# Four-layer convolution network: experts with additions to output blocks on GpSimd, the norm's pow as a step of its own, the last two block sums on VectorE, and a later third transposition

## The chip, the cores and the metric

The kernel runs on one core of one Trainium2 chip, in one launch. The metric is the device time of an execution in microseconds (us), the median of the runs. In the text PE is TensorE, DVE is VectorE, ACT is ScalarE, POOL is GpSimd, and SP is SyncE, which issues most DMAs.

## What is computed

The input x has the shape (8, 384, 32, 32) in float32. Four layers follow each other, each of the form x = x + layer(gn(x)), with gn a group norm over 32 groups of 12 channels. Layer 0 is an attention with eight heads behind depthwise projections, layer 2 a depthwise 7x7 convolution, layer 3 three fused branches. The change lies in layer 1, the experts:

```python
def _L1_conv_ref(x, gate_w, gate_b, w1, b1, w2, b2):
    E, HID, K = (4, 384, 2)
    ...
    scores = jax.nn.softmax(x_flat @ gate_w + gate_b, -1)
    top_v, top_i = jax.lax.top_k(scores, K)
    top_w = jax.nn.softmax(top_v, -1)
    wmap = top_w.T.reshape(K, b, h, w)
    present = (top_i[:, :, None] == jnp.arange(e)[None, None, :]).any(0)
    coef = jnp.einsum('ke,kbhw->ebhw', present.astype(x.dtype), wmap)
    hdn = jax.nn.relu(jnp.einsum('bchw,edc->ebdhw', x, w1) + b1[:, None, :, None, None])
    y = jnp.einsum('ebdhw,eod->ebohw', hdn, w2) + b2[:, None, :, None, None]
    return jnp.einsum('ebohw,ebhw->bohw', y, coef)
```

`present` holds, for each rank k and expert e, whether any token of the batch chose e at rank k. Where all are present, the coefficients of a token add up to one for every expert, and the output is the plain sum over the four experts. The kernel computes that sum, checks the gates, and has a second path for the other case.

## The kernel before

The experts take the eight images one after the other, each in two halves h = 0 and h = 1 of 512 tokens. In this part PE, ACT, DVE and POOL each follow the order in which the program issues their instructions, and an instruction that waits holds everything behind it on its engine. SP's DMAs are ordered by the scheduler.

A half has two parts. In the **dual part** the hidden values of three experts (e = 0, 1, 2) are made by a scheme with fewer products: a 384x384 matrix times 384x512 values is cut in 3x3 blocks of weights and 3x2 blocks of values of 256 columns, and 15 block products ("nodes", table `DUAL`) replace 18. Each node is one product (L1295, two instructions) of a sum of weight blocks (`w1sum`) and a sum of value blocks (`forms`, made by POOL at L1276 for the half after). Its result `p` lies in one of five PSUM banks, and the additions listed with the node (L1304, DVE) put it into the output blocks of `hs` or into scratch nodes, which lie in the fourth expert's slot of `hs_sum`. Nodes 14 and 10 are copied out by ACT (L1301). After nodes 6 and 5 ACT applies bias and Relu to a finished block row (`rectify`, L352). The fourth expert is done in the plain way (`classical`, L1314, ACT at L1324), its instructions strewn between the nodes.

In the **products part** the second matrix product runs over all four experts by another such scheme: 15 products (`PRODUCTS`, L1344), each accumulated over the four experts in one of the same five banks, on blocks of `hs` or on block sums (`HSUMS`, L1337), and added by DVE to two or so blocks of the residual r (L1353, L1355). The first eight block sums of `HSUMS` are made by POOL, for expert e - 1 right after the dual of expert e, for the last dual expert and the fourth at once after the dual part. The last two, over all four experts, use slots that come free in the products; they follow after product 8, on POOL for h = 0 and on DVE for h = 1 (both on DVE in the first image).

Other work is hung on the products as jobs: `jobs[i]` runs after product i is issued. In h = 0 these are the steps of `passing`, the norm of the image before (moments by `bn_stats`, L250; `centred`, L311 to L313; the group matmul, L304; `norm2`, which calls `from_moments` with four DVE steps, a pow on POOL at L332 and a step on DVE at L337; then for each of three channel tiles an affine step on ACT, a transposition on DVE at L1014, two pad copies on POOL and a store by SP), the normalizing of the next half (`normed`), the forms of the next half (`make_forms`, twelve additions on POOL) and the loads of the next image (`fetch_next`). In h = 1 they are the next image's residual (L1164), its `normed` and its forms.

The first half of the first image is different. All four experts are done in the plain way, in the order 3, 0, 1, 2, the block sums are on DVE, and POOL makes the sums of weight blocks, `WSUMS` of w2 (L1248) and then of w1 (`sum_weights`, L1262).

Of the kernel before, what the change touches and what calls it, by code (L numbers as in the profile page):

```python
# [64 lines left out]
def taps(xp, dy, dx, rows=H, h0=0):  # L65
# [72 lines left out]
    (0, (((0, 0), "p0", 9, 1),)),  # L138
    (9, ((8, 11, "p9", -1), ((0, 0), (0, 0), 11, 1))),
    (11, ((6, "p11", 9, 1), ((1, 0), (1, 0), 8, 1))),  # L140
    (8, ((3, "p8", 8, 1),)),
    (3, (((0, 1), "p3", 6, 1), ((1, 1), (1, 1), 3, 1))),
    (7, ((10, 6, "p7", -1), (10, 10, 3, 1))),
    (2, (((2, 0), "p2", 10, 1),)),
    (6, (((0, 1), (0, 1), "p6", 1), ((2, 1), "p6", 10, 1))),
    (5, (((1, 1), (1, 1), "p5", 1), ((2, 1), (2, 1), "p5", 1))),
)
NODE_AT = {n: i for i, n in enumerate((1, 9, 6, 10, 14, 11, 8, 3))}
READY = {6: (0,), 5: (1, 2)}
# [24 lines left out]
def conv_mixer_kernel(ctx: ExitStack, tc: tile.TileContext, a: dict, out: bass.AP):  # L174
# [139 lines left out]

    def from_moments(own, ps, ref, s, t, gm, first=None):

        c, n = ps.shape[1], ps.shape[3]
        both, sq = (
            own.tile([P, c, n], FP, tag=f"fm_{k}", name=f"fm_{k}") for k in "ab"
        )  # L320
        nc.vector.tensor_copy(both, ps[:, :, 0])
        nc.vector.tensor_mul(sq, both, both)
        nc.vector.scalar_tensor_tensor(
            out=sq, in0=ps[:, :, 1], scalar=EPS, in1=sq, op0=ALU.add, op1=ALU.subtract
        )
        nc.vector.tensor_add(gm, both, ref)
        for n0, n1 in ((0, first or n), (first or n, n)):
# [4 lines left out]
            nc.gpsimd.tensor_tensor(  # L332
                out=s[:, :, n0:n1], in0=sq[:, :, n0:n1], in1=half, op=ALU.pow
            )
            if n0:
                yield
            nc.vector.scalar_tensor_tensor(  # L337
                out=t[:, :, n0:n1], in0=gm[:, :, n0:n1], scalar=-1.0, in1=s[:, :, n0:n1],
                op0=ALU.mult, op1=ALU.mult,
            )  # L340
# [250 lines left out]
    def layers(again, early, xst, pre_pool, pp0, pw):  # L591
# [548 lines left out]
        def experts():  # L1140
# [100 lines left out]

            def block(n):
                if isinstance(n, tuple):
                    return w2[:, :, n[1], n[0] * P : (n[0] + 1) * P]
                return wsum[:, wslot[n]]

            for o, i, sign, j in WSUMS:
                nc.gpsimd.tensor_tensor(  # L1248
                    out=block(o), in0=block(i), in1=block(j), op=ALU.add if sign > 0 else ALU.subtract
                )  # L1250
            w1slot = {n: i for i, n in enumerate(n for n in wslot if n not in (8, 9))}
# [7 lines left out]
            def sum_weights(some):  # L1259
                for o, i, sign, j in some:  # L1260
# [4 lines left out]
                    )  # L1265

            def form_of(n, xn):
                n = PLAIN.get(n, n) if isinstance(n, int) else n
                if isinstance(n, tuple):
                    return xn[:, n[0], n[1] * QF : (n[1] + 1) * QF]  # L1270
                return forms[:, fslot[n]]

            def make_forms(xn):
                for o, i, j, sign in FORMS:
                    i, j = (form_of(v, xn) for v in (i, j))
                    nc.gpsimd.tensor_tensor(  # L1276
                        out=forms[:, fslot[o]], in0=i, in1=j,
                        op=ALU.add if sign > 0 else ALU.subtract,
                    )
# [3 lines left out]

            def dual(hs, e, xn, part, got):

# [7 lines left out]
                for n, ops in DUAL[part]:  # L1293
                    ps = got[f"p{n}"] = ep.tile([P, HF], FP, tag="p", name="p")
                    nc.tensor.matmul(  # L1295
                        ps[:, :QF], lhsT=block1(PRODUCTS[n][0])[:, e], rhs=form_of(n, xn),
                        start=True, stop=True,
                    )
                    for o, i, *more in ops:
                        if not more:  # L1300
                            nc.scalar.copy(at(o), at(i))  # L1301
                            continue
                        j, sign = more
                        nc.vector.tensor_tensor(  # L1304
                            out=at(o), in0=at(i), in1=at(j), op=ALU.add if sign > 0 else ALU.subtract
                        )
                    for m in READY.get(n, ()):
                        rectify(hs, e, m)
# [26 lines left out]
            def sums(hs, some, s, eng=nc.vector):  # L1335
                for o, i, j in some:
                    eng.tensor_add(rows_of(o, hs, s), rows_of(i, hs, s), rows_of(j, hs, s))  # L1337

            def products(b, h, hs, jobs):
                r, begun = rs[b], set()  # L1340
                for i, (w, x, outs) in enumerate(PRODUCTS):
# [36 lines left out]

            def norm2(ps, b, cos, st):
                c = slice(cos[0], cos[-1] + 1)  # L1380
                cols = [st[:, c, i : i + 1] for i in range(3)]
                for _ in from_moments(er, ps[:, c], ref2[:, c, b : b + 1], *cols):
                    pass

            def next_layer(b):
# [3 lines left out]
                if b < B - 1:  # L1389
# [21 lines left out]
                for i, (cts, co) in enumerate(zip(parts, cos)):  # L1411
# [7 lines left out]
                    yield  # L1419
                    norm2(ps, b, co, st)  # L1420
                    yield
# [29 lines left out]
            for b, h in product(range(B), range(2)):  # L1451
# [1111 lines left out]
```

## Time and profile before

| What | us |
|---|---|
| time before, median of 3 runs | 3171.03 (3170.06 to 3171.54) |
| the profiled execution's own time | 3177.68 |
| its span | 3175.9 |
| busy PE, DVE, ACT, POOL over the span | 3001.4, 1912.0, 1213.5, 787.4 |
| first and last product of the experts (L1344) | 1765.8, 2668.5 |
| DVE additions of the dual part (L1304), one | 0.40 to 0.97 |
| POOL sums of two 128x256 blocks (L1337), median | 0.73 to 0.79 |
| POOL pow (L332), median | 0.86 |
| DVE transposition (L1014), median | 1.98 |

Times of instructions and positions come from the one profiled execution, whose time lies 6.65 us above the median. In a row of the timeline the columns are start, duration, engine, line, instruction, output and inputs, and how many instructions the row joins; in brackets stands the idle time before it and what ended it. A matmul row's duration is modelled; the distance of two starts is not.

### The profile page before, as it was taken

To read this page: it belongs to the slowest core of one execution; us is meant where nothing else is said; L and a number is where in the kernel's file an instruction comes from. 1 tells how busy PE (TensorE), PEld (TensorE's weight loads), DVE (VectorE), ACT (ScalarE), POOL (GpSimd) and SP (SyncE) were. 2 spreads that over 40 slices of the span, in tenths; PEclk is the share of its full clock that TensorE was granted. 3 is DMA by queue.
4 is the path that set the end of the run, shared out by engine and by line. 5 is a ranking of instruction groups with operands and counts; after the bars stand their busy time and mean duration, and the time that the engine had idled before them with its cause. 6 is when DMAs were issued, how large, how long until landed. Compare 5 with 4: busy or idle time off the path is not lost.

```text
span 3175.9 us, 45058 instructions
## 1 busy us (share of the span) xinstructions
PE 3001.4 (95%) x18280; PEld 1696.7 (53%) x18280; DVE 1912.0 (60%) x3179; ACT 1213.5 (38%) x1446; POOL 787.4 (25%) x982
## 2 busy tenths in 40 slices
PE   4988999999999999999998999999999999887998
PEld 3765434343433334343433677777777777556543
DVE  6898354445444444445445778878877876447164
ACT  3654453535445353535342122212222223446510
POOL 2432000000000000000001565575665663111400
PEclk9999999999999999999999999999999999898999
DMA  6787011011101111011004012112112114867765
GB/s 218 270 278 288 37 38 67 23 62 43 60 25 60 43 43 62 23 62 43 13 23 163 1 40 84 44 40 84 54 39 76 51 41 143 321 221 241 235 221 188
DMA packets 89105, 323.02 MB, mean 102 GB/s; under 512 B 13608, under 2 KB 16000, under 8 KB 84664
## 3 DMA queue, kind: packets, MB, share of 16 engines
q1 hardware_dynamic: 64936, 251.71, 23.3%
q10 hardware_dynamic: 13776, 35.82, 3.6%
q0 software_dynamic: 10176, 32.51, 3.0%
q8 instruction: 146, 2.39, 0.3%
q14 instruction: 71, 0.58, 0.1%
HBM read 211.66 MB, written 111.68 MB: 102 GB/s over the span
## 4 chain that ended last, share of the span: by engine, by line
PE 74%; DVE 14%; DMA 5%; issue 3%; POOL 2%; ACT 1%; SPq 0%; ACTq 0%; DVEq 0%; POOLq 0%
PE sc L771 15%; PE av L790 14%; PE p L1344 10%; PE p L1295 8%; PE sc L669 7%; PE sc L724 4%; PE sc L846 4%; PE ph L1314 4%; DVE stats L250 3%; DVE y L499 2%; DVE hs L1304 2%; PE po L2374 1%; PE po L2377 1%; PE po L2385 1%; DVE xt L466 1%
## 5 line engine op out<-in xcount | busy, mean ns | idle before, releaser
L778 ACT ACTIVATE e<-sc 128x1024 f32<-128x1024 f32 x512 | 483.1, 1029 | 609.1 <-PE sc L771 608.9
L771 PE MATMUL sc<-qT,kT 64*128 64x512 f32 x2048 | 473.9, 602 | 0.0
L790 PE MATMUL av<-e,vT 128*64 128x512 f32 x2048 | 467.7, 598 | 0.0
L771 PEld LDWEIGHTS sc<-qT,kT 64*128 64x128 f32 x2048 | 186.7, 186 | 282.1 <-issue 231.2
L790 PEld LDWEIGHTS av<-e,vT 128*64 128x64 f32 x2048 | 135.5, 136 | 316.4 <-issue 316.4
L820 POOL DMA_DIRECT2D att<-att x45 | 23.8, 533 | 980.7 <-DVE att L815 980.7
L806 DVE LOAD_MASK_SELECT sm<-av x64 | 0.9, 14 | 417.0 <-PE av L790 417.0
L1337 POOL TENSOR_TENSOR hs_sum<-hs,hs_sum 128x256 f32<-128x256 f32 (+1 forms) x239 | 247.1, 1042 | 14.7
L669 PE MATMUL sc<-y,pw 128*128 128x512 f32 x576 | 249.3, 594 | 0.0
L528 PE MATMUL ps<-xt,wx 64*64 64x256 f32 x3456 | 197.3, 386 | 38.3 <-DVE xt L466 21.4
L808 DVE RECIPROCAL inv<-sm 128x512 f32<-128x512 f32 x64 | 214.6, 3353 | 2.2
L352 ACT ACTIVATE hs<-hs,b 128x512 f32<-128x512 f32 x135 | 89.8, 716 | 293.4 <-DVE hs L1304 293.4
L1337 POOL TENSOR_TENSOR hs_sum<-hs 128x256 f32<-128x256 f32 (+1 forms) x135 | 132.9, 1013 | 271.6 <-ACT hs L352 214.3
L528 PEld LDWEIGHTS ps<-xt,wx 64*64 64x64 f32 x3456 | 155.4, 137 | 79.1 <-issue 37.5
L1353 DVE TENSOR_TENSOR r<-r,p 128x256 f32<-128x256 f32 x416 | 152.9, 412 | 67.9 <-PE p L1344 64.7
L1295 PE MATMUL p<-forms,w 128*128 128x256 f32 x630 | 178.5, 391 | 8.4 <-DVE hs_sum L1304 6.3
L1114 PE MATMUL ps<-xt,wx 64*64 64x256 f32 (+1 forms) x2912 | 161.1, 380 | 24.9 <-ACT wx L1716 14.5
L669 PEld LDWEIGHTS sc<-y,pw 128*128 128x128 f32 x576 | 108.8, 190 | 140.0 <-issue 138.6
L1344 PE MATMUL p<-hs_sum,wsum 128*128 128x256 f32 x768 | 174.2, 380 | 0.0
L1314 PE MATMUL ph<-xn,w 128*128 128x512 f32 x342 | 159.9, 602 | 3.0 <-ACT xn L352 3.0
L1304 DVE TENSOR_TENSOR hs<-p,hs_sum 128x256 f32<-128x256 f32 x270 | 113.7, 421 | 77.5 <-PE p L1295 30.6
L1344 PEld LDWEIGHTS p<-hs_sum,wsum 128*128 128x128 f32 x768 | 145.0, 190 | 19.9
(346 smaller groups left out, 4628.3 us busy)
## 6 DMA issues: line engine op xcount, KB each, us to landing
raw<-y SPq DMA_DIRECT2D x72, 512.0 KB
y<-raw SPq DMA_DIRECT2D x24, 1536.0 KB
x<-x SPq DMA_DIRECT2D x23, 608.0 KB
xt<-x SPq DMA_DIRECT2D x23, 608.0 KB
w<-in_w ACTq DMA_DIRECT2D x36, 384.0 KB
xn<-in_x SPq DMA_DIRECT2D x24, 512.0 KB
x<-in_x SPq DMA_DIRECT2D x16, 768.0 KB
z<-z POOLq DMA_DIRECT2D x16, 768.0 KB, 4.3
```

Source lines behind the costliest of these rows:

```text
L528: nc.tensor.matmul(ps[64 * d : 64 * d + 64, 2 * i + e, cc], lhsT=w[r, 12 * cc + 6 * e + 3 * d + k, :], rhs=xt0s[ct][r, 16 * d + 4 * u + 2 ...
L669: nc.tensor.matmul(ps[:, h, :], lhsT=w[:, ct, pair, :], rhs=y[:, ct, h * HF : (h + 1) * HF], start=ct == 0, stop=ct == NC - 1,)
L771: nc.tensor.matmul(sc[:, s, :], lhsT=kTs[b][r, pair, m * P : (m + 1) * P], rhs=qTs[b][r, pair, h * HF : (h + 1) * HF], start=True, stop=True,)
L778: nc.scalar.activation(e, sc, AF.Exp, scale=1.0 if shifted else HD**-0.5)
L790: nc.tensor.matmul(av[64 * s : 64 * s + 64, :], lhsT=vTs[0][:, m, c0 : c0 + 64], rhs=e[:, s, :], start=m == 0, stop=m == N // P - 1,)
L808: nc.vector.reciprocal(inv, sm)
L1114: nc.tensor.matmul(ps[64 * d : 64 * d + 64, 2 * i + e, c % 2, images], lhsT=w[r, d * K7 + k, :], rhs=by_slot(xts[ct])[r, 16 * d + column(c ...
L1295: nc.tensor.matmul(ps[:, :QF], lhsT=block1(PRODUCTS[n][0])[:, e], rhs=form_of(n, xn), start=True, stop=True,)
L1304: nc.vector.tensor_tensor(out=at(o), in0=at(i), in1=at(j), op=ALU.add if sign > 0 else ALU.subtract)
L1314: nc.tensor.matmul(ph, lhsT=w1[:, e, ct, dc * P : (dc + 1) * P], rhs=xn[:, ct, :], start=ct == 0, stop=ct == NC - 1,)
L1337: eng.tensor_add(rows_of(o, hs, s), rows_of(i, hs, s), rows_of(j, hs, s))
L1344: nc.tensor.matmul(ps[:, :QF], lhsT=block(w)[:, e], rhs=rows_of(x, hs, e), start=e == 0, stop=e == E - 1,)
```

## The change

- `DUAL` loses three additions that read only SBUF, (0,0) += 11, (1,0) += 8 and (1,1) += 3. They stand in `ASIDE`, are issued on POOL after nodes 9, 11 and 3, and work on the expert at hand. The node order is the same.
- The eight block sums of expert e - 1 are no longer issued in one piece after the dual of expert e. A generator `sums_of` issues one of them on POOL after each of the nodes in `FILL`. Those of the last two experts stay in one piece.
- `norm2` is a generator that pauses between the pow and the step that reads it, so these are two jobs (after products 6 and 8).
- The steps of `passing` are hung on products 0, 1, 2, 3, 5, 6, 8, 10, 12 instead of 0, 1, 2, 3, 6, 7, 9, 10, 12, 14; the last one, the third transposition with its pads and store, follows the dual of expert 1 in h = 1.
- The forms of h = 1 are made in two parts, three after product 3 and nine after product 6 (behind the pow). The rest of w1's sums in the first image moves from product 4 to 7, the next image's loads from 14 to 13.
- The last two block sums are on DVE in every half.
- In the first half w1's sums are issued ahead of w2's, and DVE's block sums follow each expert by itself.

```diff
-    (9, ((8, 11, "p9", -1), ((0, 0), (0, 0), 11, 1))),
-    (11, ((6, "p11", 9, 1), ((1, 0), (1, 0), 8, 1))),
+    (9, ((8, 11, "p9", -1),)),
+    (11, ((6, "p11", 9, 1),)),
     (8, ((3, "p8", 8, 1),)),
-    (3, (((0, 1), "p3", 6, 1), ((1, 1), (1, 1), 3, 1))),
+    (3, (((0, 1), "p3", 6, 1),)),
...
+ASIDE = {9: ((0, 0), 11), 11: ((1, 0), 8), 3: ((1, 1), 3)}
+FILL = (4, 13, 1, 12, 8, 7, 6, 5)
...
-            if n0:
+            if n0 or pause:
                 yield
...
+            sum_weights(WSUMS[:8])
...
             for o, i, sign, j in WSUMS:
                 nc.gpsimd.tensor_tensor(
...
-            def make_forms(xn):
-                for o, i, j, sign in FORMS:
+            def make_forms(xn, part=slice(0, len(FORMS))):
+                for o, i, j, sign in FORMS[part]:
...
+                    if n in ASIDE:
+                        o, i = ASIDE[n]
+                        nc.gpsimd.tensor_add(at(o), at(o), at(i))
+                    if n in FILL:
+                        next(fill, None)
                     for m in READY.get(n, ()):
                         rectify(hs, e, m)
...
+            def sums_of(hs, e):
+                for some in HSUMS[:-2]:
+                    yield sums(hs, (some,), slice(e, e + 1), nc.gpsimd)
...
                     if i == 8:
-                        begun_all = b > 0 and h == 0
-                        sums(hs, HSUMS[-2:], slice(0, E), nc.gpsimd if begun_all else nc.vector)
+                        sums(hs, HSUMS[-2:], slice(0, E))
...
-                    norm2(ps, b, range(NC), st)
-                    yield
+                    yield from norm2(ps, b, range(NC), st, True)
...
-                        if e == E - 3:
-                            for s in (slice(E - 1, E), slice(0, E - 2)):
-                                sums(hs, HSUMS[:-2], s)
-                    sums(hs, HSUMS[:-2], slice(E - 2, E - 1))
-                    sum_weights(WSUMS[:8])
+                        sums(hs, HSUMS[:-2], slice(e, e + 1))
...
-                        dual(hs, e, xn, slice(2, len(DUAL)), got)
-                        if e:
-                            sums(hs, HSUMS[:-2], slice(e - 1, e), nc.gpsimd)
+                        fill = sums_of(hs, e - 1) if e else iter(())
+                        dual(hs, e, xn, slice(2, len(DUAL)), got, fill)
+                        if (h, e) == (1, 1) and passing:
+                            next(passing, None)
...
-                        for i in (0, 1, 2, 3, 6, 7, 9, 10, 12, 14):
+                        for i in (0, 1, 2, 3, 5, 6, 8, 10, 12):
                             at(i, next, passing)
                     at(2, normed, b, 1)
-                    at(3, lambda b=b: make_forms(xns[b, 1]))
+                    at(3, lambda b=b: make_forms(xns[b, 1], slice(0, 3)))
+                    at(6, lambda b=b: make_forms(xns[b, 1], slice(3, len(FORMS))))
                     if b == 0:
-                        at(4, sum_weights, WSUMS[8:])
+                        at(7, sum_weights, WSUMS[8:])
                     if b + 1 < B:
-                        at(14, fetch_next, b + 1)
+                        at(13, fetch_next, b + 1)
```

More of the change, by code (lines that the diff above doesn't have):

```diff
@@ L313, in centred, with from_moments @@
         nc.vector.tensor_add(o[:, :, 1], o[:, :, 1], var)
-    def from_moments(own, ps, ref, s, t, gm, first=None):
+    def from_moments(own, ps, ref, s, t, gm, first=None, pause=False):
         c, n = ps.shape[1], ps.shape[3]
@@ L1240, in experts @@
             lg = ew.tile([P, NT, E], FP, name="lg")
[L1242 to L1250, printed above, removed]
             w1slot = {n: i for i, n in enumerate(n for n in wslot if n not in (8, 9))}
@@ L1265, in sum_weights, with block @@
                     )
+            sum_weights(WSUMS[:8])
+            def block(n):
+                if isinstance(n, tuple):
+                    return w2[:, :, n[1], n[0] * P : (n[0] + 1) * P]
+                return wsum[:, wslot[n]]
+            for o, i, sign, j in WSUMS:
+                nc.gpsimd.tensor_tensor(
+                    out=block(o), in0=block(i), in1=block(j), op=ALU.add if sign > 0 else ALU.subtract
+                )
             def form_of(n, xn):
@@ L1282, in rectify, with dual @@
                 affine(hs[:, m, e], hs[:, m, e], 1.0, b1[:, e, m : m + 1], AF.Relu)
-            def dual(hs, e, xn, part, got):
+            def dual(hs, e, xn, part, got, fill=iter(())):
                 def at(n):
@@ L1377, in centred2, with norm2 @@
                 )
-            def norm2(ps, b, cos, st):
+            def norm2(ps, b, cos, st, pause=False):
                 c = slice(cos[0], cos[-1] + 1)
                 cols = [st[:, c, i : i + 1] for i in range(3)]
-                for _ in from_moments(er, ps[:, c], ref2[:, c, b : b + 1], *cols):
-                    pass
+                return from_moments(er, ps[:, c], ref2[:, c, b : b + 1], *cols, pause=pause)
             def next_layer(b):
@@ L1419, in next_layer @@
                     yield
-                    norm2(ps, b, co, st)
+                    for _ in norm2(ps, b, co, st):
+                        pass
                     yield
```

## The prediction

> **What bounds the kernel now.** I read the page first: the busy line and the slices.
>
> ```profile
> span 3175.9 us, 45058 instructions
> PE 3001.4 (95%) x18280; PEld 1696.7 (53%) x18280; DVE 1912.0 (60%) x3179; ACT 1213.5 (38%) x1446; POOL 787.4 (25%) x982
> PE   4988999999999999999998999999999999887998
> DVE  6898354445444444445445778878877876447164
> POOL 2432000000000000000001565575665663111400
> ```
>
> PE sets the pace nearly everywhere. The change lies in slices 22 to 33 (the experts, 1730 to 2670 us), where DVE has digits of 7 and 8 and POOL of 5 to 7. Only PE's idle time can be won there. One image takes (2643.54 - 1944.44) / 6 = 116.52 us (starts of the piece "PE p L1344 x116" in the chain of work). The windows view of one such image:
>
> ```profile
> 1976.00:2092.00 116.00, 112.74 (x495) 86.88 (x495) 91.29 (x203) 27.72 (x46) 71.85 (x81) 1.00 0.19 57
> ```
>
> PE (first pair) looks busy for 112.74, but ends are modelled, so I count starts. Instructions on 256 columns start every 0.216 us (24 from 2072.30 to 2077.48), on 512 columns every 0.43. An image has 2 x 15 products of 8 (51.8), 2 x 45 dual products of 2 (38.9), 2 x 18 classical instructions (15.5), logits 1.43, the group matmul 1.48, the two transpositions 0.22: 109.3 us. So PE loses about 7.2 us an image. Which waits these are, PE's own waits in 1730 to 2700 say (total, times, longest):
>
> ```profile
> PE p L1344 <- DVE r L1353: 8.7, 7, 1.3
> PE p L1295 <- DVE hs_sum L1304: 6.3, 15, 0.4
> PE p L1344 <- ACT hs L352: 6.2, 15, 0.4
> PE p L1344 <- DVE r L1355: 2.6, 1, 2.6
> ```
>
> PE's timeline places them, as the excess of each stretch over its count of starts:
>
> ```profile
> 1777.17 5.41 PE L1344 MATMUL p<-hs_sum,w 128*128 128x256 f32 x16 [2.62 <-DVE r L1355]
> 1988.06 0.70 PE L1295 MATMUL p<-forms,w 128*128 128x256 f32 x2 [0.42 <-DVE hs_sum L1304]
> 2010.97 1.62 PE L304 MATMUL gn_ps<-dq,gmatA 128*128 128x2 f32 x14
> 2024.31 1.97 PE L1344 MATMUL p<-hs_sum,w 128*128 128x256 f32 x8 [1.26 <-DVE r L1353]
> 2060.97 4.58 PE L1344 MATMUL p<-hs,w 128*128 128x256 f32 x20 [0.42 <-ACT hs L352]
> ```
>
> Dual part of h=0: 1969.80 to 1998.20 is 28.4 against 27.2 counted, 1.2 lost, all in experts 1 and 2; expert 0, without block sums on POOL beside it, loses nothing. Products of h=0: 29.6 against 27.4, 2.3 lost: 0.7 before expert 2's rectified block, 1.4 at 2024.31. Dual part of h=1: 31.7 against 28.8, 2.9 lost: 1.4 in expert 0, 1.5 in experts 1 and 2. Products of h=1: 0.7, again the rectified block. Sum 7.0.
>
> DVE and POOL show why:
>
> ```profile
> 1986.71 0.96 DVE L1304 TENSOR_TENSOR hs<-hs,hs_sum 128x256 f32<-128x256 f32 x1
> 2009.36 1.19 DVE L313 TENSOR_TENSOR dq<-dq,gn_mv 128x3 f32<-128x3 f32 x1
> 2021.20 2.31 DVE L337 SCALAR_TENSOR_TENSOR st<-st 128x3 f32<-128x3 f32 x1 [4.94 <-POOL st L332]
> 2033.37 1.98 DVE L1014 STREAM_TRANSPOSE x<-xn 128x1024 f32<-128x1024 f32 x1
> ```
> ```profile
> 1982.06 2.10 POOL L1337 TENSOR_TENSOR hs_sum<-hs 128x256 f32<-128x256 f32 x3 [12.31 <-ACT hs L352]
> 1984.23 4.02 POOL L1337 TENSOR_TENSOR hs_sum<-hs,hs_sum 128x256 f32<-128x256 f32 x5
> 2020.30 0.87 POOL L332 TENSOR_TENSOR st<-fm_b,mhalf 128x3 f32<-128x3 f32 x1
> 2021.14 4.79 POOL L1337 TENSOR_TENSOR hs_sum<-hs,hs_sum 128x1024 f32<-128x1024 f32 x2
> ```
>
> In experts 1 and 2 the three additions to output blocks take DVE 0.59, 0.61 and 0.96 us instead of 0.42, because both inputs lie in SBUF while POOL adds. DVE's expert lasts 9.44 us (1982.27 to 1991.71), PE's 8.2. At 2016 to 2021 DVE stands 4.94 us for a pow that is queued on POOL behind all twelve forms, then 2.31 us on a 128x3 step behind POOL's 128x1024 sum: PE has no free bank, and its fourteenth product no sum, until 2024.31. The third transposition ends at 2035.35, when dual work has been waiting since 2033.3.
>
> **The change part by part.**
>
> *Additions to POOL.* Per expert DVE loses three instructions: 16 x 0.34 = 5.4 us remain for 13 nodes that PE makes in 5.6. Expert 0 of h=0, which kept PE free of stalls with 19 uncontended instructions, is the nearest row: I take 0 for these stalls (1.2 + 1.5). DVE is also done sooner, so ACT's rectified block is there 1 us before PE asks: the 0.7 twice an image goes too. What is queued: POOL's eight sums took 6.19 us (1982.06 to 1988.25), 0.77 each; eleven take 8.5 against PE's 8.2. POOL starts 2.3 us behind PE's end of the expert before and falls back by 0.3. DVE's last addition to (1,1) now waits for POOL's: due at 2.3 + 8 x 0.77 = 8.5 us after that end, while DVE reaches it at 9.0 (node 3 is done at 7.0, five additions of 0.34 to 0.5 follow). Nothing is late; bounds: 0 to 1 us per expert on DVE, which five banks cover up to 1.3.
>
> The Trainium skill, "GPSIMD Engine Reference", section 4.1 "Engine selection", advises VectorE for elementwise additions, GpSimd being about half as fast for two inputs. By that rule alone the three additions would cost 3 x 0.82 instead of 3 x 0.41, and the edit would lose; the rows have 0.73 to 0.80 on POOL against 0.59 to 0.96 on a DVE that is the late one.
>
> *Pow as its own step, forms in two parts.* pow now stands behind three forms (2.4 us) instead of twelve (9), and its reader comes two products later: DVE's wait of 4.94 and most of the 2.31 go, and with them 1.4 on PE.
>
> *Last two sums on DVE.* For h=0 2.9 us on DVE (the h=1 row, 2076.62 to 2079.51, also beside forms). DVE's products of h=0 then hold 10.7 (32 additions) + 4.5 (moments) + 2.6 + 1.6 + 2.9 + 4.0 (two transpositions) = 26.3 against PE's 27.4, banks in hand: hidden. If that cover is gone, it costs up to 2.9 less the slack of 1.1, 1.8 an image. The Trainium skill, "SBUF — State Buffer", section "Who interferes with whom", says that of a DVE instruction with two SBUF inputs and a GpSimd one the later is held for the whole of the earlier. By it each of the two sums may hold a form by 1.4 us. In the row, at 2076.81, two forms took 1.61 and 1.59 us instead of 0.73; the forms held are read 6 us later, so I cost this at nothing.
>
> *Third transposition after expert 1 of h=1.* DVE has there about 1.5 us between its experts and 1.3 more before PE's banks run out; 1.98 us fits. POOL's two pad copies (0.28 each) push expert 2's block sums back by 1.3 us; the final sums still begin 2.5 us after the products do, before 3.3. SP's store of that piece goes behind the next image's loads, with half an image to spare. The 1.4 in expert 0 goes, since ACT and DVE are free when it starts.
>
> *Group matmul one product earlier* (job 5 instead of 6): a new wait. DVE's chain from the first addition to the end of L313 is 2000.81 to 2010.47, 9.7 us; starting 1.85 after the products begin it ends at 11.5. PE comes there after 6 x 1.73 = 10.4. L312 and L313 each wait for POOL's running 128x512 sum; by how its boundaries fall the pair takes 1.3 to 2.4 us. So PE waits 0 to 1.4 us; I take 0.9.
>
> *First image.* Sums expert by expert, and w1's sums ahead of w2's on a POOL that idles until 1739.6: POOL ends near 1760 instead of 1767.7, so the last experts' sums on DVE run uncontended (0.35 instead of 0.9 to 1.4 each) and end near 1770 instead of 1776.3: the 2.6 us at 1777.17 go. Its second half loses 2.1 in all (55.4 from 1798.69 to 1854.07 against 53.3); 1.9 go.
>
> **Sum.** Per image 7.0 - 0.9 - 0.4 (small remainders of 0.1) = 5.7; seven images 39.9; first image 2.6 + 1.9: 44 us. The profiled execution took 3177.68 (span 3175.9 and 1.8 around it) and should become 3133; the median, 6.65 lower, becomes 3171 - 44 = 3127.
>
> **The rivals.**
> 1. POOL is held to the order of the dual and half the gain goes into new waits: the 0.9 is 1.4, DVE's 1.8 in the products shows, and 0.5 of each dual part stays. Against it: every one of these has slack above. Gain 7.0 - 1.4 - 1.8 - 1.0 = 2.8 an image, 20 and 3 for the first: 3148.
> 2. POOL paces the experts, and the kernel is slower. From expert 0's rectified block 19 POOL instructions must be done before PE reaches expert 2's block (1,0), 18.7 us later: allowed 0.98 us each, and the gain is gone at 1.14. At 1.2 each half is late by 4.1 us, 15 halves 61, less 44: 3188. For it: POOL's 128x512 sums took 1.90 instead of 1.25 beside DVE's residual steps (2062.84). Against it: with DVE busy in the same dual part they took 0.70 to 0.80, and DVE was the one held.
> 3. The steps only change places, PE's losses stay: 3171. Against it: rows name DVE and POOL as the late ones.
>
> **How the numbers follow.** Forecast 0.76 (3115 with no new wait, 53 to 56 us gained, to 3137 with 1.4 and 1 us left elsewhere), rival 1 0.14 (3137 to 3158), rival 2 0.06, rival 3 0.04. A measurement of this kernel tells 0.2%, 6.3 us. Range 3114 to 3148; faster 0.90, same 0.04, slower 0.06.
>
> **What would show it.** Right: the image's period near 110.8; no PE wait for DVE hs_sum L1304, none before the fourteenth product; a PE wait for dq of about 1 us, seven times; DVE's st step without POOL ahead of it; POOL's sums in the dual at 0.7 to 0.8. Wrong: PE waits for POOL's block sums or ACT's rectified blocks (rival 2), or for DVE's r in h=0 (rival 1).

## The result, and the profile after

The changed kernel takes 3129.79 us (median of 4 runs, 3127.23 to 3131.61) against 3171.05 us (3170.06 to 3171.54): a ratio of 0.987, with a 95% interval of 0.9853 to 0.9887. The gain is 41.3 us; forecast were 44 us, to 3127. The profiled execution took 3131.1 us with a span of 3129.4, which is 46.5 less than the span before. The profile of before lay 6.65 us above its median and this one 1.3, so 5.3 of the 46.5 belong to the executions and not to the change.

The page of the changed kernel (span, busy time, slices):

```profile
span 3129.4 us, 45250 instructions
PE 2978.0 (95%) x18280; PEld 1710.8 (55%) x18280; DVE 1857.4 (59%) x3066; ACT 1211.5 (39%) x1446; POOL 858.7 (27%) x1103
DVE  6898344445454445444445777777777776457164
POOL 2432000000000000000000577686777764111400
```

POOL has 121 instructions more and DVE 113 fewer. In the slices of the experts DVE's digits of 8 became 7, and POOL rose from mostly 5 and 6 to 6 and 7. Note where POOL stands now: in half of these slices its digit equals DVE's.

PE's own waits from 1730 to 2660, in the changed kernel (total, times, longest). Of the four groups before, none is left; this is the only one in its place:

```profile
PE gn_ps L306 <- DVE dq L315: 6.6, 8, 2.9
```

One of the eight, the 2.9, belongs to another norm at the start of the window. The other seven are the new wait that was forecast, 0.53 us each. The 2.62 us of the first half and the 1.26 before the fourteenth product are gone. PE's timeline of the changed kernel around a group matmul:

```profile
1994.01 1.70 PE L306 MATMUL gn_ps<-dq,gmatA 128*128 128x2 f32 x14 [0.53 <-DVE dq L315]
1995.57 2.83 PE L1357 MATMUL p<-hs_sum,w 128*128 128x256 f32 x8
1998.19 6.22 PE L1357 MATMUL p<-hs_sum,wsum 128*128 128x256 f32 x24
```

Look at the second line by its starts: its eight instructions need 1.73 us, and the next line starts 2.62 later. The 24 behind them take 6.05 instead of 5.18 (the line behind them starts at 2004.24). That is 1.76 us lost while PE waits for nothing. The windows of 2 us tell why (PE, PEld, DVE, ACT, POOL busy with their counts, then the granted clock, DMA share and GB/s):

```profile
1996.00:1998.00 2.00, 2.00 (x8) 1.64 (x7) 0.00 (x0) 0.00 (x0) 1.21 (x2) 0.63 0.00 0
1998.00:2000.00 2.00, 2.00 (x6) 1.53 (x6) 1.22 (x6) 0.00 (x0) 0.28 (x1) 0.51 0.00 0
2000.00:2002.00 2.00, 2.00 (x11) 1.77 (x10) 0.42 (x1) 0.00 (x0) 2.00 (x4) 1.00 0.00 0
```

From 1996.5, 0.97 us after the group matmul has ended, the granted clock is half for 3.41 us, and it returns by itself. This happens in five of the seven images. In the other two the same wait has no such sequel, as in the next image (the eight instructions behind the group matmul take 1.81 us to the next start, 2109.35):

```profile
2105.98 1.69 PE L306 MATMUL gn_ps<-dq,gmatA 128*128 128x2 f32 x14 [0.53 <-DVE dq L315]
2107.54 1.97 PE L1357 MATMUL p<-hs_sum,w 128*128 128x256 f32 x8
```

The prediction has no term for the slow stretch. The last section says what decides between the two cases.

DVE and POOL in the same half of the changed kernel:

```profile
1992.48 1.18 DVE L314 TENSOR_TENSOR dq<-dq 128x3 f32<-128x3 f32 x1
2003.39 3.38 DVE L1346 TENSOR_TENSOR hs_sum<-hs,hs_sum 128x1024 f32<-128x1024 f32 x2
2006.69 0.68 DVE L339 SCALAR_TENSOR_TENSOR st<-st 128x3 f32<-128x3 f32 x1
```
```profile
1967.64 2.10 POOL L1346 TENSOR_TENSOR hs_sum<-hs 128x256 f32<-128x256 f32 x3 [3.25 <-ACT hs L354]
1973.43 2.21 POOL L1346 TENSOR_TENSOR hs_sum<-hs,hs_sum 128x256 f32<-128x256 f32 x3
```

The eleven POOL instructions of an expert end 8.0 us after they begin, 0.73 each. DVE's step that reads pow (L339) waits for nobody and takes 0.68 (before: 4.94 of standing and then 2.31); DVE's last two sums take 3.38.

Where the span went, by starts. The group matmul is one product, 1.73 us, earlier in the changed kernel, and two rows are corrected for it:

| stretch | before | after | difference |
|---|---|---|---|
| start to the first plain product of the experts | 1732.54 | 1730.42 | -2.1 |
| from there to the first group matmul | 161.89 | 151.62 | -10.3 (-8.5 corrected) |
| six images, group matmul to group matmul | 699.11 | 668.50 | -30.6 |
| last group matmul to the end | 582.36 | 578.86 | -3.5 (-5.2 corrected) |

An image takes 110.3 us in two cases and 111.97 in the others, where the clock falls; the mean is 111.42, against 116.52 before.

### The profile page after: what moved, and what is told of

The parts are those of the page before. It is cut to its first block, busy times and chain, and to the rows that moved or that the text cites. A ratio compares the mean times of both kernels' runs of the same rounds, so it can differ in the third digit from the quotient of the medians.

```text
span 3129.4 us, 45250 instructions
## 1 busy us (share of the span) xinstructions
PE 2978.0 (95%) x18280; PEld 1710.8 (55%) x18280; DVE 1857.4 (59%) x3066; ACT 1211.5 (39%) x1446; POOL 858.7 (27%) x1103
## 5 line engine op out<-in xcount | busy, mean ns | idle before, releaser
L1346 POOL TENSOR_TENSOR hs_sum<-hs,hs_sum 128x256 f32<-128x256 f32 (+1 forms) x225 | 209.7, 940 | 9.4
L530 PEld LDWEIGHTS ps<-xt,wx 64*64 64x64 f32 x3456 | 156.8, 137 | 76.1 <-issue 39.7
L1299 PE MATMUL p<-forms,w 128*128 128x256 f32 x630 | 165.4, 379 | 0.0
L1116 PEld LDWEIGHTS ps<-xt,wx 64*64 64x64 f32 x2912 | 109.2, 139 | 73.3 <-ACT wx L1725 15.1
```

The costliest lines, as they stand in the source:

```text
L530: nc.tensor.matmul(ps[64 * d : 64 * d + 64, 2 * i + e, cc], lhsT=w[r, 12 * cc + 6 * e + 3 * d + k, :], rhs=xt0s[ct][r, 16 * d + 4 * u + 2 ...
L1116: nc.tensor.matmul(ps[64 * d : 64 * d + 64, 2 * i + e, c % 2, images], lhsT=w[r, d * K7 + k, :], rhs=by_slot(xts[ct])[r, 16 * d + column(c ...
L1299: nc.tensor.matmul(ps[:, :QF], lhsT=block1(PRODUCTS[n][0])[:, e], rhs=form_of(n, xn), start=True, stop=True,)
```

## The experiments

All kernels were timed in three rounds beside the kernel before, whose median on those chips was 3172.3 to 3173.3. "Image" is the distance of two group matmuls in the profile.

The table has the four parts of an image, by starts of PE's instructions in the profiles (us, images 2 to 8). In italics stand the values of images with half clock behind the group matmul.

| kernel | dual, h = 0 | products, h = 0 | dual, h = 1 | products, h = 1 |
|---|---|---|---|---|
| before | 28.6 | 29.6 | 31.7 | 26.6 |
| changed | 27.15 | 28.2, *29.9* | 29.0 | 25.9 |
| 1: additions back on DVE | 28.6 | 29.7, *31.3 to 33.0* | 30.7 | 26.0 |
| 3: group matmul later | 27.15 | 27.5 | 29.0 | 25.9 |
| 5: pow and forms back | 27.15 | 28.3, *29.9* | 29.8, *29.0* | 25.9 |
| 11: additions alone | 27.15 | 30.2 | 29.7 to 30.1 | 25.9 |
| 12: additions, sums, first half | 27.15 | 29.2 | 30.9 | 25.9 |

In run 11 one image is left out of the row: half clock before its fourteenth product makes its products 31.9 and its dual part of h = 1 29.0.

**1. The additions back on DVE**, the rest of the change kept.

```diff
-                        nc.gpsimd.tensor_add(at(o), at(o), at(i))
+                        nc.vector.tensor_add(at(o), at(o), at(i))
```

> The changed kernel with one part undone: the three additions to output blocks of each expert go back to VectorE, at the same nodes; all else stays. Theory (VectorE's lateness in experts 1 and 2 was the largest loss, and moving the additions removed it): the losses of the dual parts come back, 1.2 us in h=0, 1.5 in h=1, and 0.7 twice an image ahead of the rectified block, 4.1 us x 7 images and about 2 in the first, some 30 us: 3160 us, with PE waiting for DVE hs_sum again. Rival (the gain came from the norm steps and the last sums, the dual parts would have caught up anyway): 3130 us, no such wait.

Measured 3170.83, ratio 0.9996 (0.9986 to 1.0007): the whole gain is lost, more than was expected. Image 115.0 to 118.4. PE's waits in this kernel:

```profile
PE p L1299 <- DVE hs_sum L1308: 7.4, 22, 0.4
PE p L1357 <- ACT hs L354: 3.3, 8, 0.4
```

These are two of the four groups of before, by the same names: DVE late in the dual part, and the rectified block behind it. The wait before the group matmul grew as well (9.0 us in seven, longest 1.3), and the half clock with it, now in six of seven images. So the 41 us are not the additions' alone. By the table the rest of the change still shortens the two parts of h = 1 by 1.5 us an image, and the earlier group matmul, with a later DVE ahead of it, lengthens the products of h = 0 by 1.9 in the mean. On balance the rest is worth nothing while DVE is late.

**2. The block sums in one piece**, after the dual of each expert as before.

```diff
-                        dual(hs, e, xn, slice(2, len(DUAL)), got, fill)
+                        dual(hs, e, xn, slice(2, len(DUAL)), got)
+                        if e:
+                            sums(hs, HSUMS[:-2], slice(e - 1, e), nc.gpsimd)
```

> The changed kernel with the block sums of expert e - 1 again in one piece of eight after the dual of expert e, the additions still on GpSimd. Theory (GpSimd has slack of several us before the products read its sums): the final sums begin about 4 us after the products instead of 1.7, the first of them is read 8.6 us after, so no wait of PE: 3130 us, within 3. Rival (the spreading is what keeps GpSimd from pacing; a piece of 6.2 us in front of the next expert's additions holds VectorE's last addition and the rectified blocks): 0.5 to 1 us per expert in 2 experts of 15 halves, 3145 to 3160 us, with PE waiting for ACT hs or POOL hs_sum.

Measured 3121.55, ratio 0.9838 (0.9821 to 0.9854): not slower but some 8 us faster than the changed kernel. Image 109.96. There is no wait in the dual parts, so strewing the sums between the nodes buys nothing. The wait at the group matmul is 0.37 us by starts instead of 0.70, and the clock stays at full in all images, so an image is 1.46 us shorter than the changed kernel's mean. DVE's chain ahead of it ends earlier because its step L313 takes 0.16 us here and 0.43 in the changed kernel: here it begins between two of POOL's 128x512 sums (1993.17, where the sums start at 1991.86 and 1.31 us apart), there in the middle of one. Nothing in the edit aims at that; it is luck of the order.

**3. The group matmul one product later**, where it was before.

```diff
-                        for i in (0, 1, 2, 3, 5, 6, 8, 10, 12):
+                        for i in (0, 1, 2, 3, 6, 7, 8, 10, 12):
...
-                    at(6, lambda b=b: make_forms(xns[b, 1], slice(3, len(FORMS))))
+                    at(7, lambda b=b: make_forms(xns[b, 1], slice(3, len(FORMS))))
```

> The changed kernel with the group matmul after product 6 instead of 5, norm2's first part and the nine forms after product 7 instead of 6; its reader stays after product 8. In the changed kernel PE waits 0.53 us for dq ahead of the group matmul, seven times, and in five of the seven images the granted clock then falls to about 0.5 for some 3.4 us (the two stretches after it take 1.7 us longer). Theory (wait and slow clock go together: wait and group matmul make 2.1 us of little work on PE, without the wait 1.5, as in the kernel before, where the clock stayed at 1.00): both go, 7 x 0.53 + 5 x 1.7 = 12 us: 3118 us, clock 1.00 in every image. Rival A (the slow clock comes from something else, such as the rest of the stage running without idle time): only the wait goes, 3126 us. Rival B (norm's later steps now push VectorE beyond the products): 3130 us or more, with PE waiting for DVE r.

Measured 3121.15, ratio 0.9841 (0.9825 to 0.9858). Of this group of PE's waits only the other norm's 2.9 us is left. Every image takes 109.51 us; the prediction's count of starts was 109.3. This is the best version that was run, 8.6 us below the median of the changed kernel. The intervals of the two ratios overlap by a little, and the profiles say where the time goes: the spans differ by 13.5 us, of which 0.70 x 7 = 4.9 are the wait and five slow stretches of 1.7 are 8.5. (The profiled execution of run 3 is its fastest, 3117.66, so the spans differ by more than the medians.)

**4. A product in the wait.** One unused 128x256 product is issued ahead of each group matmul into a part of the same PSUM tile that nothing reads. It needs no result of DVE, so PE works where it stood.

```diff
-                    ps = eh.tile([P, NC, 2, 1], FP, tag="sm", name="gn_ps")
+                    room = eh.tile([P, HF], FP, tag="sm", name="gn_ps")
+                    nc.tensor.matmul(
+                        room[:, QF:], lhsT=w2[:, 0, 0, :P], rhs=xns[b + 1, 0][:, 0, :QF],
+                        start=True, stop=True,
+                    )
+                    ps = room[:, : NC * 2].rearrange("p (c k n) -> p c k n", k=2, n=1)
```

> The changed kernel with one product of two 128x256 instructions (0.43 us), whose result nobody reads, put on PE ahead of each of the seven group matmuls, in the time in which PE waits 0.53 us. Theory (the idle time ahead of the small matmuls makes the clock fall): the wait shrinks to 0.1 us, the stretch of little work to 1.6 us, the clock stays up, 5 x 1.7 = 8.5 us less: 3121 us. Rival (the small matmuls themselves, or the instant at which they run, make it fall): the useless product hides in the wait and changes nothing, 3130 us, five images with a slow stretch.

Measured 3121.59, ratio 0.9844 (0.9827 to 0.986), with one product (two instructions) more per image and nothing taken away. PE's timeline:

```profile
1992.32 0.59 PE L1410 MATMUL gn_ps<-xn,w 128*128 128x256 f32 x2
1994.51 1.97 PE L1357 MATMUL p<-hs_sum,w 128*128 128x256 f32 x8
```

The eight instructions behind the group matmul now take 1.81 us to the next start (1996.32) where the changed kernel's took 2.62. Image 110.24. The slow stretch thus follows from PE having nothing to do just ahead of the small matmuls, and not from the small matmuls alone: the kernel before had them too, with no gap ahead, at full clock in all seven images.

**5. Pow and forms back**: pow and its reader in one step, the twelve forms in one piece after product 3, with the group matmul in its new, earlier place.

```diff
-                    yield from norm2(ps, b, range(NC), st, True)
+                    for _ in norm2(ps, b, range(NC), st):
+                        pass
+                    yield
...
-                    at(3, lambda b=b: make_forms(xns[b, 1], slice(0, 3)))
-                    at(6, lambda b=b: make_forms(xns[b, 1], slice(3, len(FORMS))))
+                    at(3, lambda b=b: make_forms(xns[b, 1]))
```

> The changed kernel with pow and its reader in one step again (after product 6) and all twelve forms after product 3, so that pow stands behind twelve forms on GpSimd; all else stays. Theory (that order made VectorE stand 4.94 us and cost PE 1.4 us an image): VectorE stands 4 to 5 us after product 6, its last two sums and the transpositions come 4 us later, PE waits 1 to 2 us ahead of the fourteenth product or in the next dual part: 7 x 1 to 2 us, 3137 to 3145 us. Rival (with VectorE relieved elsewhere, its wait for pow is covered): 3130 us, no new wait of PE.

Measured 3133.49, ratio 0.9879 (0.9846 to 0.9912); image 112.0, and 111.1 in one. Five of seven have half clock behind the group matmul, as in the changed kernel. DVE does stand again, as this line of its timeline shows:

```profile
2006.18 0.16 DVE L339 SCALAR_TENSOR_TENSOR st<-st 128x3 f32<-128x3 f32 x1 [4.25 <-POOL st L334]
```

PE stops for it only twice in seven images:

```profile
PE p L1299 <- DVE r L1366: 1.1, 2, 0.5
```

But these two are just the two images at full clock, and by starts each loses 0.8 us in the dual part of h = 1 (table). In the other five PE has already lost 1.7 us to half clock, and DVE has caught up by then. So the run does not show that the stall is covered: behind a PE at full clock pow's place is worth 0.8 us an image, with the additions on POOL. The theory's 1 to 2 us was too much, the rival's nothing too little.

**6. The third transposition after product 14 again.**

```diff
-                        if (h, e) == (1, 1) and passing:
-                            next(passing, None)
...
-                        for i in (0, 1, 2, 3, 5, 6, 8, 10, 12):
+                        for i in (0, 1, 2, 3, 5, 6, 8, 10, 12, 14):
```

> The changed kernel with the third transposition back after product 14. In the changed kernel VectorE ends the products of h=0 at 2016.5 and its first dual addition waits for PE until 2018.65, and the third transposition needs 1.9 us. Theory (the 1.4 us in expert 0 came from the late pow ahead of it, not from the transposition's place): it fits, 3130 us, period unchanged at 110.3 or 112.0. Rival (its place was worth the 1.4 us): 7 x 1.4, 3140 us, with PE waiting in expert 0 of h=1.

Measured 3131.54, ratio 0.9871 (0.9851 to 0.9891), images of 110.3 and 111.95 as in the changed kernel (one of 112.27, where the wait before the group matmul is 0.3 us longer), and no new wait, in the two images at full clock either. Its place is worth nothing here.

**7. The last two sums of h = 0 on POOL** again.

```diff
-                        sums(hs, HSUMS[-2:], slice(0, E))
+                        sums(hs, HSUMS[-2:], slice(0, E), nc.gpsimd if b > 0 and h == 0 else nc.vector)
```

> The changed kernel with the last two block sums of h=0 back on GpSimd (images 1 to 7). Theory (GpSimd is busy with forms until about 26 us after the products begin, two sums of 2.4 us follow, and the fourteenth product wants the first of them at 26): PE waits 2.5 to 4.5 us ahead of products 13 and 14, and a wait that long may bring the slow clock too: 7 x 2.5 to 5, 3147 to 3165 us, PE waiting for POOL hs_sum. Rival (either engine does): 3130 us.

Measured 3139.55, ratio 0.9896 (0.9871 to 0.9921): 9.8 us above the changed kernel (8 by the ratios, whose intervals overlap). Image 111.7 to 113.4. PE waits for these sums:

```profile
PE p L1357 <- POOL hs_sum L1346: 4.5, 11, 0.5
```

By starts it is 0.57 + 0.72 = 1.3 us an image, before the two products that read them. So the edit that the prediction costed at nothing, and credited with nothing, is worth about 1.3 with the rest of the change in place.

**8. The first half's old order.** Block sums and sums of weight blocks as before the change:

```diff
-            sum_weights(WSUMS[:8])
-
...
-                        sums(hs, HSUMS[:-2], slice(e, e + 1))
+                        if e == E - 3:
+                            for s in (slice(E - 1, E), slice(0, E - 2)):
+                                sums(hs, HSUMS[:-2], s)
+                    sums(hs, HSUMS[:-2], slice(E - 2, E - 1))
+                    sum_weights(WSUMS[:8])
```

> The changed kernel with the first half of the first image as it was (sums of w1's blocks behind those of w2's, VectorE's block sums of experts 3, 0 and 1 together). Theory (that part was worth the 2.6 us of PE's wait and the slow stretch behind it, in which 16 instructions took 5.25 us instead of 3.45): 4.4 us more, 3134 us, PE waiting 2.6 us for DVE r in the sixth product. Rival (the time comes back later in that half): 3130 us.

Measured 3133.72, ratio 0.9879 (0.9857 to 0.9901), 3.9 us above the changed kernel. The intervals overlap, so the times alone do not show it. The profile has 2.9 us of waiting for DVE's r and 1.78 us of half clock behind it, 4.7 in all. The kernel before had the same: after its 2.62 us of waiting the sixteen instructions took 5.25 us where 3.45 are counted.

**9 and 10. More on POOL**: one, and then two, unused additions of 128x256 ahead of each moved one, so 14 and 17 POOL instructions per expert instead of 11. They change no output.

```diff
+            spare = ew.tile([P, QF], FP, name="spare")
...
+                        for _ in range(1):
+                            nc.gpsimd.tensor_add(spare, xn[:, 0, :QF], xn[:, 1, :QF])
                         nc.gpsimd.tensor_add(at(o), at(o), at(i))
```

(`range(2)` in the second.)

> The changed kernel with three more additions of 128x256 on GpSimd in each of the three dual experts, one ahead of each of the moved additions, into a tile that nobody reads. It asks how much slack GpSimd has (rival 2 of the prediction: 19 instructions must be done within 18.7 us). In the changed kernel an expert's eleven take 8.0 us (1967.64 to 1975.64), 0.73 each. Theory (deadline of 18.7 us): 19 + 5 = 24 x 0.73 = 17.5 us, still inside: same as the changed kernel, 3130 us, PE without waits in the dual parts. Rival (GpSimd is already at its limit, any addition shows): 2 x 2.2 us a half, 15 halves, 3195 us.

> The same with six more additions in each dual expert, two ahead of each moved one. Theory (deadline of 18.7 us): 19 + 10 = 29 x 0.73 = 21.2 us, 2.5 us too late in each half, 15 x 2.5 = 37 us: 3165 us, with PE waiting for DVE hs_sum or hs in expert 2 and for ACT hs ahead of the products. If GpSimd has more slack than that: 3130 us.

Measured 3167.35, ratio 0.9984 (0.9974 to 0.9994), and 3265.81, ratio 1.0303 (1.0286 to 1.032). Three more cost 37 us, which eats the gain, and six more 136; over 15 halves that is 2.5 and 9 us each. The first lies between theory (3130) and rival (3195), the second far above its theory (3165). Half clock has a part in it: the profiles have 31 and 75 us of it between 1755 and 2645 us, against 17 in the changed kernel. The path in the kernel with three more (DVE's timeline, then PE's):

```profile
1980.84 0.75 DVE L1309 TENSOR_TENSOR hs<-hs,p 128x256 f32<-128x256 f32 x2 [1.50 <-POOL hs L1316]
```
```profile
1982.94 0.70 PE L1300 MATMUL p<-xn,w 128*128 128x256 f32 x2 [0.59 <-ACT hs_sum L1306]
```

DVE's last additions wait for POOL's (1,1) += 3, ACT's Relu waits for DVE, ACT's copies of nodes 14 and 10 stand behind that Relu, and PE waits for the bank that the copy frees. POOL is at work on one expert's fourteen without a pause from 1972.92 to 1982.95 and goes straight on to the next expert's. Fourteen instructions of 0.73 are 10.2 us against PE's 8.2 an expert, and the delay is passed on from expert to expert.

**11. The additions alone**, in the kernel before: `ASIDE` and its three additions, nothing else.

```diff
+                    if n in ASIDE:
+                        o, i = ASIDE[n]
+                        nc.gpsimd.tensor_add(at(o), at(o), at(i))
```

> The kernel before with one part of the change alone: the three additions of each expert on GpSimd, at the same nodes; block sums in one piece, group matmul after product 6, pow behind twelve forms, last two sums of h=0 on GpSimd and the first half as before. Prediction's attribution (the additions are worth 1.2 + 1.5 + 1.4 an image): 29 us less for seven images and 2 in the first: 3140 us, with 1.4 us lost ahead of the fourteenth product and 1.4 in expert 0 of h=1. What the runs so far suggest (with VectorE relieved, pow's place and the third transposition's cost nothing, and only the last sums on GpSimd still do, about 1.4 us): an image of 109.5 + 1.4 = 110.9 us, 5.6 less, 39 and 2 in the first: 3130 us.

Measured 3149.48, ratio 0.993 (0.9914 to 0.9947): 23 of the 41 us. Image 113.0 to 113.4 (one 113.96). The waits in the dual parts and for the rectified blocks are gone, and one has grown (PE's timeline):

```profile
1901.00 1.97 PE L1348 MATMUL p<-hs_sum,w 128*128 128x256 f32 x8 [2.54 <-DVE r L1357]
```

Before the fourteenth product 2.7 us are lost instead of 1.4, and in the next dual part mostly 0.7 of some 1.2 in expert 0 are still lost. Together that is 3.5 us against 2.6 before. So the additions alone do not remove the lateness that pow causes, they add to it: with eleven instead of eight instructions an expert POOL comes later to the final sums and the forms, and pow starts 10.62 us after the group matmul (1897.00 less 1886.38) instead of 9.33 (1903.77 less 1894.43 in the kernel before). DVE stands 6.30 us for it (4.94 before), then 2.29 on the 128x3 step.

**12. The additions, the last two sums and the first half**, in the kernel before; the pow, the forms, the group matmul and the third transposition stay where they were.

```diff
+                    if n in ASIDE:
+                        o, i = ASIDE[n]
+                        nc.gpsimd.tensor_add(at(o), at(o), at(i))
...
-                        begun_all = b > 0 and h == 0
-                        sums(hs, HSUMS[-2:], slice(0, E), nc.gpsimd if begun_all else nc.vector)
+                        sums(hs, HSUMS[-2:], slice(0, E))
...
+                        sums(hs, HSUMS[:-2], slice(e, e + 1))
```

> The kernel before with three parts of the change: the additions on GpSimd, the last two block sums on VectorE in every half, and the first half's new order. Left out are the spreading of the block sums, the pause at pow, the two parts of the forms, the earlier group matmul and the later third transposition. What the runs so far suggest (the parts left out are worth nothing, and the earlier group matmul costs 1.9 us an image): an image of 109.5 to 110.0 us, 47 to 50 us less than before, 3121 to 3124 us, PE without waits. Prediction's attribution (pow's place and the transposition's are worth 1.4 us each): 2.8 us an image lost, 3141 us.

Measured 3140.74, ratio 0.9902 (0.9886 to 0.9919), 11 us above the changed kernel and 19.6 above the best one. Image 113.1. PE's waits, and DVE's line behind them:

```profile
PE p L1350 <- DVE hs_sum L1343: 10.1, 7, 1.5
PE p L1298 <- DVE r L1359: 9.2, 7, 1.3
```
```profile
2010.53 0.16 DVE L338 SCALAR_TENSOR_TENSOR st<-st 128x3 f32<-128x3 f32 x1 [6.31 <-POOL st L333]
```

The last two sums are DVE's own now, yet they start late, because DVE stands for pow: 1.6 us are lost before the fourteenth product, and 1.5 at the second node of the next dual part. That is ahead of the third transposition (one such wait ends at 2018.02, the transposition starts at 2022.75), so it too comes from pow; some 0.3 more follow behind the transposition. Run 5 lost 0.8 us at full clock and run 6 nothing, each with one of the two edits undone; with pow, forms, group matmul and transposition all as before, 3.6 us an image are lost against run 3. They stand in for each other in part.

## Why the prediction was right

The sign, the mechanism and nearly the sum held: 41.3 us against 44, 5.1 us an image against 5.7. That the sum came so near is in part luck, as the steps show:

- **The count.** 109.3 us an image was right: with no wait and full clock, run 3 has 109.51. The remainder was 0.2 where 0.4 was taken.
- **Additions to POOL.** Forecast: dual parts free of stalls and the two 0.7 before rectified blocks gone. All are gone, at 0.73 per POOL instruction where 0.77 was taken. It is the core of the gain: 23 us alone, and without it the rest of the change gains nothing on balance. By itself it is worth 3.3 us an image (116.5 to 113.25), less than the 4.1 credited, because the longer queue on POOL makes pow 1.3 us later (run 11).
- **Pow and the third transposition.** The prediction gave 1.4 to each. The losses did go, and the additions alone do not remove them (run 11). But the split is not as it was worked out: in the changed kernel the transposition's place is worth nothing (run 6) and pow's 0.8 in images at full clock (run 5), while with all four of the norm's steps as before 3.6 come back, most of it ahead of the transposition (run 12). The working took each edit by itself against the state of before; several of them remove the same lateness of DVE, and pow behind the forms is its main source.
- **Last two sums on DVE.** Costed at nothing and hidden, which is right, at 3.38 us instead of 2.9. What was missed is that it is also a gain: with the rest of the change, POOL's sums come 1.3 us late (run 7).
- **Group matmul earlier.** The new wait came where it was put, 0.70 us by starts, within 0 to 1.4, where 0.9 was taken. What failed is that the sum stops at the wait: the clock behind it costs 1.7 us in five images of seven, 1.2 in the mean. That term was missing. It is twice the 0.6 an image by which the forecast was too high; the other half is offset by smaller errors the other way (0.2 each in the wait, in the remainder and in the total of 7.0, which the starts put at 7.2). Wait and clock together eat nearly all that the products of h = 0 gain: they are 0.2 us shorter than before in the mean, where 2.3 less 0.9 was expected.
- **First image.** The 2.6 went, and with it 1.8 of half clock that the prediction's own trace held: the count of starts of those sixteen instructions, 5.25 against 3.45, would have shown it. Here the missing clock term made the forecast too low, and so it makes up for a part of the other miss.
- **Rivals.** Rival 1's new waits in the products and the dual did not come. Rival 3 is excluded by the time. Rival 2 did not come about, but its point was placed wrongly. It allowed POOL 18.7 us for 19 instructions; at 0.73 even 25 would be in time, and run 9, whose 14 per expert make it 25, loses 2.5 us a half. The allowance counted POOL's work up to one block of the third expert that PE reads late, and left out that DVE's last addition waits for POOL, that ACT's Relu and copies queue behind DVE, and that PE waits for the bank behind the copies. The margin lies between 11 instructions an expert (8.0 us of PE's 8.2) and 14 (10.2).

Three things stay open. No run moves pow alone in the kernel before, so what it is worth there is not measured. The 2.1 us ahead of the experts belong to no step of the change; executions of one kernel differ by as much. And the times of the changed kernel spread over 4.4 us. A varying number of slow stretches would fit, since run 8, with the same later images, has four where the changed kernel has five; but the mean granted clocks of the four executions (0.979, 0.979, 0.979 and 0.980, the last for the slowest) do not follow their times, so the cause is not shown.

## What to carry to other kernels

Where the engine that lags shares a stage with an idle one, move the instructions that have no reader close behind them, and compare the receiver's load per step with the pace of the step: 8.0 of 8.2 us was free of waits, 10.2 lost the whole gain. Follow each moved instruction through every in-order queue that it can now hold (here POOL, DVE, ACT, PE), since such a chain of waits hands its delay on from round to round. When parts of a change are undone one at a time, look whether another loss hides what the part was worth, as half clock did in run 5. A step that is put earlier to save time can cost more than its wait: ask what TensorE's clock does behind the gap, and try the later place.

## What the runs showed of the hardware

- A short gap can halve TensorE's clock. In the changed kernel 0.70 us of standing and then 1.55 us of fourteen 128x2 matmuls, 2.25 us of little work, are followed by 3.41 us at a granted clock of 0.5 in five of seven images (1.7 us lost each), in run 1, with 1.45 us of standing, in six of seven. With 0.37 us of standing (run 2), none (run 3, before) or a product in the gap (run 4) it does not happen. A gap of 2.5 us before the fourteenth product (run 11) did it in one image of seven.
- A grid of time decides which. In each of the fourteen traces all stretches at 0.5 begin on one grid of 3.413 us, to within 2 ns (in the changed kernel at 1883.896, 1996.536, 2218.403, 2331.042 and 2552.909, which are 33, 65, 33 and 65 steps apart). What counts is how much little work falls into one step. In the five slow images of the changed kernel at least 2.19 of the 2.25 us do; in the other two the grid cuts the stretch, and no step has more than 1.78. In run 10 a longer stretch, 2.84 us, is cut to at most 1.97 in four of six images, and they stay at full clock. Counting 0.216 us for 256 columns and 0.43 for 512 as work and the rest as little work (an estimate from starts), between 1745 and 2625 us in all traces all 59 steps at full clock with at least 2.12 us of little work are followed by half clock, and none with 2.07 or less.
- The Trainium skill, "TensorE: Matmul & The Clock Gate", section "Why this matters for your kernels", warns of idle gaps of more than about 3 us between bursts of matmuls. The slow stretch of 3.41 us is as long as the window that the same page describes in its Part 1, "The HAM clock gate"; the gap that sufficed was shorter, 2.25 us, and two thirds of it were filled with small matmuls. Here the measurement decides.
- A 128x3 step with two SBUF inputs on DVE takes as long as the POOL sum beside it has left: 0.16 to 0.17 us alone, 1.18 beside a 128x512 sum, 2.3 beside a 128x1024 one. In the dual parts POOL's own 128x256 additions stayed at 0.72 to 0.92 us. They are not always the ones that go first: beside DVE's two 128x1024 sums two of POOL's forms took 1.70 us each instead of 0.72 (changed kernel, 2003.99 and 2005.65), and no wait of PE came of it.
